# Graph attention on one core: scores of the first 32 tiles in groups of four instead of two

## The chip, the cores and the metric

The kernel runs on one core of one Trainium2 chip. The metric is the device time of one execution in microseconds (us). A core has a matrix engine (TensorE, PE in the profile; its weight loads are listed as PEld), a vector engine (DVE), an activation engine (ACT), GpSimd (POOL) and a queue that issues transfers (SP). Each takes its instructions in the order in which the program lists them, and they wait for one another by semaphores. Matrix products are accumulated in PSUM, which the program uses as eight banks of 128 partitions by 512 float32.

## The reference, cut to what matters

One graph attention layer with pre-normalisation, 384 nodes, 1024 features, 16 heads of 64:

```python
h = relu(layernorm(x))
q = h @ wq.T + bq;   k = h @ wk.T + bk;   v = h @ wv.T + bv
q2 = heads(q @ wiq.T + biq);  k2 = heads(k @ wik.T + bik);  v2 = heads(v @ wiv.T + biv)
scores = einsum('hnd,hmd->hnm', q2, k2) / 8 + mask        # mask from the edges, -inf elsewhere
out = einsum('hnm,hmd->hnd', softmax(scores), v2)
y = x + out.reshape(384, 1024) @ wo.T + bo
```

Everything is asked for in float32. The kernel makes each product out of three products of split operands: high part times high part, high times low, low times high.

## The kernel before, in words

The first part (up to about 158 us) makes the normalised input, the first projections, the mask and v2. The second part, which the change touches, is one loop over steps `i` from 0 to 59, written out by hand: the order in which the loop calls its functions is the order of the instructions on every engine. No scheduler moves them.

A **tile** is 128 rows of the scores of one head against all 384 columns. There are 48: head pair `p` (0 to 7), row block `t` (0 to 2), head `o` of the pair (0 or 1), so tile `i` has `p, r = divmod(i, 6)`, `t = r // 2`, `o = r % 2`. A tile passes through these functions:

- `do_S(i)`, in even steps, makes the scores of tiles `i` and `i+1` on PE: three product terms for two heads, six matmuls. A head has only 64 features, so its matmul uses 64 of the 128 rows of the array, and the two heads use the two halves (the profile writes 64\*128 for this form). The two results go to two banks of the tag "s", of which there are four, taken in turn.
- `do_ttr` (DVE, line 974) adds the mask out of the bank, writes the tile `e` and the row minimum. When it is done the bank is free. Step `i` calls it for tile `i-1`.
- `do_exp` (ACT) in step `i` for tile `i-2`; `do_recip` (DVE, then POOL); `do_high` (ACT, line 1009) for tile `i-5` and `do_low` (DVE, line 1013) for tile `i-6` make the two half-precision planes `pl`; `do_turn` transposes them by a transfer on the SP queue into `pt`.
- `av_mm(p)` (PE, line 1037) multiplies six turned tiles with v2: 18 matmuls that use 64 of the 128 columns of the array (128\*64). It is called in the steps of `a_at`: 14, 20, 26, ..., 50, 54. Where scores are made in that step it follows them directly, otherwise it comes later in the step.

PE's remaining time in the loop is filled by `fill`, which draws ordinary matmuls from two generators: the projections that make `iq` and `ik` of the next head pairs (lines 494 to 496, three matmuls to a piece; float16 operands for `iq`, 32-bit operands for `ik`), and later the output projection. Each step has a budget `r` in matmuls, `(STEP - costs of what the step does itself) / UNIT`; half is drawn ahead of `do_S`, half behind it. `STEP` is 1.94, `UNIT` 0.168, the cost of a score group `SMM` 0.7 and of `av_mm` `AMM` 1.69. The weights for these pieces are split on ACT, DVE (lines 118, 125, 127) and POOL (line 113) as the generators reach new chunks; the finished chunks are moved out of PSUM by ACT (lines 803, 807), DVE (804, 808) and POOL (809).

Of the kernel before, what the change touches and what calls it, by code (L numbers as in the profile page):

```python
# [19 lines left out]
N, D, NT, KT, NP = 384, 1024, 3, 8, 8  # L20
# [7 lines left out]
def gnn_kernel(ctx: ExitStack, tc: tile.TileContext, x, edges, erows, etw, wq, wk, wv, wiq, wik, wiv, wo,  # L28
# [6 lines left out]
    nc = tc.nc  # L35
# [14 lines left out]
    def bank(tag):  # L50
        return psum.tile([128, 512], F32, tag=tag, name=tag, bufs={"g": 3, "s": 4}.get(tag, 1))
# [742 lines left out]
    qk = {}  # L794
# [18 lines left out]
    def run_later():  # L813
        todo = later[:]
        later.clear()
        for f in todo:
            f()

    def run_tasks():
        while tasks:  # L820
            tasks.pop(0)()
# [54 lines left out]
    PRE, STEP, UNIT, SMM, AMM = 90, 1.94, 0.168, 0.7, 1.69  # L876
# [8 lines left out]
    def wo_prep(k):  # L885

        dst = None
        if k == 4:
            otile[0] = gtile("g3").rearrange("p a k n -> p (a k n)")
        if 4 <= k < 7:  # L890
            g, b = otile[0], (k - 4) * 2048
            dst = g[:, b:b + 2048]
        split_hi(WO + k, dst, k in ODVE)
        later.append(lambda: later.append(lambda: split_lo(WO + k)))
        load(WO + k + 3)
# [19 lines left out]
    def flush_y(n=6):  # L915
        for _ in range(min(n, len(ysums))):
            ysum(ysums.pop(0))
# [29 lines left out]
    def in_dma(i):  # L947
        return i < S - 2

    def tile_of(i):  # L950
        p, r = divmod(i, 6)
        return p, r // 2, r % 2

    st_ps, es, sts, tps, avs, aof = {}, {}, {}, {}, {}, {}
    S = 48
    TERMS = ((0, 0), (1, 0), (0, 1))

    def do_S(i):
        p, t, _ = tile_of(i)
        q, k = qk["iq", p], qk["ik", p]  # L960
        pair = [bank("s") for _ in range(2)]
        for j, (a, b) in enumerate(TERMS):
            for o in range(2):
                r = slice(o * 64, o * 64 + 64)
                nc.tensor.matmul(pair[o][:, :N], q[r, a, t * 128:(t + 1) * 128], k[r, b, :], start=(j == 0), stop=(j == 2))  # L965
        st_ps[i], st_ps[i + 1] = pair

    def do_ttr(i):
        t = tile_of(i)[1]
        e = es[i] = work.tile([128, N], F32, tag="e", name="e", bufs=EB)  # L970
        if i % 2 == 0:
            sts[i // 2] = work.tile([128, 6], F32, tag="s", name="s", bufs=5)
        s = sts[i // 2]
        nc.vector.tensor_tensor_reduce(e, st_ps.pop(i)[:, :N], ma[:, t, :], neg_c, 3.0e38, OP.add, OP.min,  # L974
                                       s[:, i % 2:i % 2 + 1])

    def do_exp(i):
        s, o = sts[i // 2], i % 2
        nc.scalar.activation(es[i], es[i], AF.Exp, bias=s[:, o:o + 1], scale=-1.0, accum_out=s[:, 2 + o:3 + o])  # L979
# [11 lines left out]
    def do_recip(i):  # L991
        s = sts[i // 2]
        nc.vector.reciprocal(s[:, 4:6], s[:, 2:4])  # L993
        if in_dma(i):
            nc.gpsimd.tensor_scalar(s[:, 4:6], s[:, 4:6], PSC, None, op0=OP.mult)  # L995

    def do_norm(i):
        if not in_dma(i):
            nc.gpsimd.tensor_tensor(es[i], es[i], factor(i).to_broadcast([128, N]), OP.mult)
# [7 lines left out]
    def do_high(i):  # L1007
        planes[i] = work.tile([128, 2, N], F16, tag="pl", name="pl", bufs=5)
        nc.scalar.activation(planes[i][:, 0, :], es[i], AF.Copy, scale=factor(i))  # L1009

    def do_low(i):
        pl = planes[i]
        nc.vector.scalar_tensor_tensor(pl[:, 1, :], es.pop(i), factor(i), pl[:, 0, :], op0=OP.mult, op1=OP.subtract)  # L1013

    def do_turn(i):
        pt, c = pt_of(i)
        nc.sync.dma_start_transpose(pt[:, :, c], planes.pop(i).rearrange("p a n -> p (a n)"))

    def turn_mm(i):
        ps = tps[i] = bank("s")  # L1020
        for k in range(3):
            nc.tensor.transpose(ps[:, k * 128:(k + 1) * 128], es[i][:, k * 128:(k + 1) * 128], ident)

    def do_pt(i):
        pt, c = pt_of(i)
        hi, lo = (pt[:, s * 3:s * 3 + 3, c] for s in range(2))
        pv = tps.pop(i)[:, :N].rearrange("p (k n) -> p k n", k=3)
        nc.scalar.activation(hi, pv, AF.Copy, scale=PSC)
        later.append(lambda: nc.vector.scalar_tensor_tensor(lo, pv, PSC, hi, op0=OP.mult, op1=OP.subtract))

    def av_mm(p):
        ps = avs[p] = bank("a")
        for k in range(3):
            for j, (sv, sp) in enumerate(TERMS):
                for o in range(2):
                    h = 2 * p + o
                    nc.tensor.matmul(ps[o * 64:o * 64 + 64, :N], vhl[:, k, h, sv, :], ptv[h % 4][:, 3 * sp + k, :],  # L1037
                                     start=(k == 0 and j == 0), stop=(k == 2 and j == 2))

    def do_ao(p):  # L1040
        f = aof[p] = work.tile([128, 512], F32, tag="aof", name="aof", bufs=3)[:, :N]
        nc.scalar.activation(f, avs.pop(p)[:, :N], AF.Identity, scale=0.5 / PSC, bias=bias_ao[:, p:p + 1])

    def do_aos(p):
        nc.vector.tensor_copy(ao[:, 0, p, :], aof[p])
        nc.gpsimd.tensor_tensor(ao[:, 1, p, :], aof[p], ao[:, 0, p, :], OP.subtract)
# [4 lines left out]
    def fill(n):  # L1051
        credit[0] += n
        while credit[0] > 0 and gens:
            try:
                c = next(gens[0])
            except StopIteration:
                gens.pop(0)
                continue
            if c == 0:
                credit[0] = 0.0  # L1060
                return
            credit[0] -= c
# [6 lines left out]
    t_at = {i + 5: i for i in range(S) if not in_dma(i)}  # L1069
    a_at = {6 * p + 14 if p < 7 else 54: p for p in range(8)}  # L1070
    for i in range(S + 12):
        now[0] = i
        scores = i < S and i % 2 == 0
        r = (STEP - SMM * scores - AMM * (i in a_at) - 0.33 * (i in t_at)) / UNIT
        fill(r / 2)
        if scores:
            do_S(i)
            if i in a_at:
                av_mm(a_at[i])
        fill(r / 2)  # L1080
        for o in range(2):
            x = i - LAGL[o]
            if x % 2 == o and 0 <= x < S and in_dma(x):
                do_low(x)
        if 0 <= i - 1 < S:
            do_ttr(i - 1)
        run_later()
        if 0 <= i - 2 < S:
            do_exp(i - 2)
        if 0 <= i - 3 < S and i % 2 == 0:  # L1090
            do_recip(i - 3)
            for x in (i - 4, i - 3):
                do_norm(x)
        for o in range(2):
            x = i - LAGH[o]
            if x % 2 == o and 0 <= x < S and in_dma(x):
                do_high(x)
        if i in t_at:
            turn_mm(t_at[i])
        if i in a_at and not scores:  # L1100
            av_mm(a_at[i])
        if i - 1 in t_at:
            do_pt(t_at[i - 1])
        if i - 1 in a_at:
            do_ao(a_at[i - 1])
        if i - 2 in a_at:
            do_aos(a_at[i - 2])
        run_tasks()
        for f in steps.pop(i, []):
            f()  # L1110
        for o in range(2):
            x = i - LAGT[o]
            if x % 2 == o and 0 <= x < S and in_dma(x):
                do_turn(x)
        if i in WSTEPS:
            wo_prep(wp)
            wready[wp] = i + 3
            wp += 1
        flush_y()
# [58 lines left out]
```

## Time and profile before

| | us |
|---|---|
| time, median of 3 runs | 277.41 (276.87 to 277.54) |
| the profiled execution's own time | 275.86 |
| its span, first to last instruction | 273.7 |
| PE busy | 267.6 |
| DVE busy | 230.5 |
| ACT busy | 215.2 |
| POOL busy | 136.7 |
| granted TensorE clock | 1.000 of full |

The profiled execution was 1.55 us shorter than the median of the runs; 2.16 us of its time lie outside the span. In the profile a row of the timeline gives start, duration, engine, line, operation, what is written from what, and how many instructions are merged into the row. Matmuls overlap, so the time that one takes on PE is read from its start to the next one's start, not from its duration. "64\*128 64x384 f16" means that 64 rows and 128 columns of the array are used, with an operand of 64 partitions by 384 elements in float16. Where an engine stood idle before an instruction, the row ends with that time and with what ended it.

### The profile page before, as it was taken

How to read it: one execution, taken by the hardware profiler on the slowest of the kernel's cores; microseconds unless marked ns; L12 is line 12 of the kernel's file. 1: busy time of each engine (PE TensorE's matmuls, PEld its weight loads, DVE VectorE, ACT ScalarE, POOL GpSimd, SP SyncE). 2: the span in 40 equal slices, each digit the busy share in tenths (PEclk: the TensorE clock that was granted, in tenths of full speed). 3: DMA queues.
4: the chain of work that ended last, by engine and by line, in shares of the span. 5: the costliest groups of instructions: out<-in, count | busy, mean ns of one | idle time of the engine just before them, and what ended most of it. 6: DMA issues, size and time to landing. Idle time of an engine off the chain costs nothing.

```text
span 273.7 us, 5038 instructions
## 1 busy us (share of the span) xinstructions
PE 267.6 (98%) x1626; PEld 186.9 (68%) x1626; DVE 230.5 (84%) x564; ACT 215.2 (79%) x417; POOL 136.7 (50%) x161
## 2 busy tenths in 40 slices
PE   7899999999999999999999999999999999999994
PEld 6899999999974444566668767766576664444543
DVE  4858986999999976798997899989988898999633
ACT  3797687599896977899968599979989899888400
POOL 4765754645778564868960005656574512212410
PEclk9999999999999999999999999999999999999999
DMA  7899999889989999396899953799899989999406
GB/s 257 267 299 406 387 397 392 323 282 403 369 261 355 383 312 341 104 379 250 288 375 393 411 209 119 172 206 211 168 240 164 216 197 167 201 174 136 86 14 219
DMA packets 58090, 72.05 MB, mean 263 GB/s; under 512 B 41040, under 2 KB 42576, under 8 KB 58064
## 3 DMA queue, kind: packets, MB, share of 16 engines
q1 hardware_dynamic: 56000, 69.93, 83.9%
q0 software_dynamic: 2064, 1.80, 2.1%
q8 instruction: 13, 0.21, 0.3%
q14 instruction: 13, 0.11, 0.1%
HBM read 59.27 MB, written 3.39 MB: 229 GB/s over the span
## 4 chain that ended last, share of the span: by engine, by line
PE 94%; DMA 2%; DVE 2%; ACT 0%; issue 0%; SPq 0%
PE g L494 24%; PE g L496 23%; PE g L495 23%; PE s L965 5%; PE a L1037 5%; PE s L494 3%; PE s L496 3%; PE s L495 3%; DMA g<-in_x_dram 2%; PE g L598 2%; PE a L495 1%; PE a L494 1%; PE a L496 1%; DVE whl L125 1%; DVE lnt L374 0%; ACT whl L102 0%
## 5 line engine op out<-in xcount | busy, mean ns | idle before, releaser
L494 PE MATMUL g<-g,whl 128*128 128x384 f32 (+1 forms) x248 | 85.3, 344 | 0.0
L496 PE MATMUL g<-g,whl 128*128 128x384 f32 (+1 forms) x248 | 82.6, 333 | 0.0
L495 PE MATMUL g<-g,whl 128*128 128x384 f32 (+1 forms) x248 | 82.5, 333 | 0.0
L351 POOL DMA_INDIRECT tab<-edge x51 | 61.9, 1213 | 37.5 <-DMA tab<-edge 23.5
L102 ACT ACTIVATE whl<-raw,small 128x1024 f16<-128x1024 f32 (+1 forms) x36 | 34.6, 970 | 3.9 <-DVE small L573 3.1
L494 PEld LDWEIGHTS g<-g,whl 128*128 128x128 f32 x184 | 34.5, 188 | 4.1 <-issue 3.1
L1013 DVE SCALAR_TENSOR_TENSOR pl<-e,s,pl 128x384 f16<-128x384 f32 x46 | 31.4, 683 | 7.0 <-ACT pl L1009 7.0
L125 DVE SCALAR_TENSOR_TENSOR whl<-raw,small,whl 128x1024 f16<-128x1024 f32 x24 | 32.8, 1368 | 4.6 <-ACT whl L102 3.6
L495 PEld LDWEIGHTS g<-g,whl 128*128 128x128 f32 x184 | 34.6, 188 | 0.0
L496 PEld LDWEIGHTS g<-g,whl 128*128 128x128 f32 x184 | 34.5, 188 | 0.0
L979 ACT ACTIVATE e<-e,s 128x384 f32<-128x384 f32 x48 | 29.1, 606 | 2.6 <-DVE s L974 2.5
L974 DVE CUSTOM_DVE_ANT_0 e<-s,ma,small 128x384 f32<-128x384 f32 x48 | 29.2, 608 | 0.0
L1009 ACT ACTIVATE pl<-e,s 128x384 f16<-128x384 f32 x46 | 27.8, 605 | 1.8 <-POOL s L995 1.7
L108 ACT ACTIVATE whl<-raw 128x1024 fp32r<-128x1024 f32 (+1 forms) x30 | 25.2, 847 | 2.4 <-DMA raw<-in_wik_dram 1.3
L995 POOL TENSOR_SCALAR s<-s 128x2 f32<-128x2 f32 x23 | 9.0, 393 | 34.4 <-DVE s L993 34.4
L127 DVE TENSOR_TENSOR whl<-raw,whl 128x1024 fp32r<-128x1024 f32 x17 | 21.0, 1237 | 2.4 <-ACT whl L108 2.1
L113 POOL TENSOR_TENSOR whl<-raw,whl 128x256 fp32r<-128x256 f32 x20 | 17.0, 858 | 9.3 <-issue 6.2
L155 ACT ACTIVATE scan<-scan 128x1024 f32<-128x1024 f32 x20 | 20.9, 1043 | 0.0
L494 PE MATMUL g<-hk,whl 128*128 128x384 f16 x64 | 20.9, 326 | 0.0
L495 PE MATMUL g<-hk,whl 128*128 128x384 f16 x64 | 20.9, 326 | 0.0
L496 PE MATMUL g<-hk,whl 128*128 128x384 f16 x64 | 20.9, 326 | 0.0
L809 POOL TENSOR_TENSOR ik<-f,ik 128x384 f16<-128x384 f32 x7 | 6.4, 913 | 28.2 <-DVE ik L808 23.6
(196 smaller groups left out, 552.0 us busy)
## 6 DMA issues: line engine op xcount, KB each, us to landing
raw<-in_wv_dram SPq DMA_DIRECT2D x8, 512.0 KB
raw<-in_wq_dram SPq DMA_DIRECT2D x8, 512.0 KB
scan<-in_wiv_dram SPq DMA_DIRECT2D x8, 512.0 KB
raw<-in_wiv_dram SPq DMA_DIRECT2D x8, 512.0 KB
scan<-in_wk_dram SPq DMA_DIRECT2D x8, 512.0 KB
raw<-in_wk_dram SPq DMA_DIRECT2D x8, 512.0 KB
g<-in_wo_dram SPq DMA_DIRECT2D x8, 512.0 KB
raw<-in_wiq_dram SPq DMA_DIRECT2D x8, 512.0 KB
```

What stands on the lines that cost most here:

```text
L102: soon(j if parts > 1 else -1, lambda c=c: nc.scalar.activation(hi[:, c], raw[w][:, c], AF.Copy, scale=sc))
L108: soon(j if parts > 1 else -1, lambda c=c: nc.scalar.activation(hi[:, c], raw[w][:, c], AF.Copy))
L125: nc.vector.scalar_tensor_tensor(lo, raw[w], sc, hi, op0=OP.mult, op1=OP.subtract)
L127: (eng or nc.vector).tensor_tensor(lo, raw[w], hi.bitcast(F32), OP.subtract)
L351: nc.gpsimd.indirect_dma_start(out=tabs[c // RNG], out_offset=bass.IndirectOffsetOnAxis(ap=idx[:, c:c + 1], axis=0), in_=val[:, c:c + 1], ...
L494: nc.tensor.matmul(ps, lhi, rhi, start=first, stop=False)
L495: nc.tensor.matmul(ps, lhi, rlo, start=False, stop=False)
L496: nc.tensor.matmul(ps, llo, rhi, start=False, stop=last)
L974: nc.vector.tensor_tensor_reduce(e, st_ps.pop(i)[:, :N], ma[:, t, :], neg_c, 3.0e38, OP.add, OP.min, s[:, i % 2:i % 2 + 1])
L979: nc.scalar.activation(es[i], es[i], AF.Exp, bias=s[:, o:o + 1], scale=-1.0, accum_out=s[:, 2 + o:3 + o])
L1009: nc.scalar.activation(planes[i][:, 0, :], es[i], AF.Copy, scale=factor(i))
L1013: nc.vector.scalar_tensor_tensor(pl[:, 1, :], es.pop(i), factor(i), pl[:, 0, :], op0=OP.mult, op1=OP.subtract)
```

## The change

For the first 32 tiles the scores are made in groups of four tiles, in every fourth step: twelve matmuls in a row into all four "s" banks. From tile 32 on nothing differs in the group size. For the first 32 tiles `do_ttr` is called one step earlier (tile `i` in step `i`); step 32 has none, and from step 33 on it is tile `i-1` again. The budget of `fill` is adapted in these steps: 0.05 less a step, and 0.49 more for a score group.

```diff
+    QUADS = 32
+
     def do_S(i):
-        p, t, _ = tile_of(i)
-        q, k = qk["iq", p], qk["ik", p]
-        pair = [bank("s") for _ in range(2)]
-        for j, (a, b) in enumerate(TERMS):
-            for o in range(2):
-                r = slice(o * 64, o * 64 + 64)
-                nc.tensor.matmul(pair[o][:, :N], q[r, a, t * 128:(t + 1) * 128], k[r, b, :], start=(j == 0), stop=(j == 2))
-        st_ps[i], st_ps[i + 1] = pair
+        for x in range(i, i + (4 if i < QUADS else 2), 2):
+            p, t, _ = tile_of(x)
+            q, k = qk["iq", p], qk["ik", p]
+            pair = [bank("s") for _ in range(2)]
+            for j, (a, b) in enumerate(TERMS):
+                for o in range(2):
+                    r = slice(o * 64, o * 64 + 64)
+                    nc.tensor.matmul(pair[o][:, :N], q[r, a, t * 128:(t + 1) * 128], k[r, b, :], start=(j == 0), stop=(j == 2))
+            st_ps[x], st_ps[x + 1] = pair
...
-        scores = i < S and i % 2 == 0
-        r = (STEP - SMM * scores - AMM * (i in a_at) - 0.33 * (i in t_at)) / UNIT
+        scores = i < S and i % (4 if i < QUADS else 2) == 0
+        r = (STEP - (i < QUADS) * 0.05 - (SMM + 0.49 * (i < QUADS)) * scores - AMM * (i in a_at) - 0.33 * (i in t_at)) / UNIT
         fill(r / 2)
         if scores:
             do_S(i)
...
-        if 0 <= i - 1 < S:
+        if i < QUADS:
+            do_ttr(i)
+        elif QUADS < i <= S:
             do_ttr(i - 1)
```

## The prediction

> **What bounds the kernel now.** I read the page first: the share of each engine and the chain that ended last.
>
> ```profile
> span 273.7 us, 5038 instructions
> ...
> PE 267.6 (98%) x1626; PEld 186.9 (68%) x1626; DVE 230.5 (84%) x564; ACT 215.2 (79%) x417; POOL 136.7 (50%) x161
> ...
> PE 94%; DMA 2%; DVE 2%; ACT 0%; issue 0%; SPq 0%
> ```
>
> PE is busy for 98% of the span and is 94% of the chain: whatever shortens PE's sequence shortens the run, as long as no other engine makes PE wait. The view of waits tells whether one does now.
>
> ```profile
> PE g L435 <- POOL ident masks.py:199: 1.4, 1, 1.4
> PE g L415 <- DVE g L407: 0.8, 1, 0.8
> PE s L415 <- ACT g L403: 0.2, 1, 0.2
> PEld L965 <- issue: 7.4, 24, 0.4
> ```
>
> PE's only named waits are three at the very start. None is for a score bank, for weights or for a turned tile. But its weight loads stood idle ahead of every one of the 24 score groups, 7.4 us in all, "until issue", so for nothing another engine did. Third, the share of the other engines in the stretch of the first 32 tiles:
>
> ```profile
> 160.00:216.00 56.00, 56.00 (x380) 37.30 (x379) 50.85 (x133) 50.80 (x120) 30.36 (x41) 1.00 0.89 188
> ```
>
> The columns are the stretch, its length, then busy time of PE, PEld, DVE, ACT, POOL, the clock, the DMA share and GB/s. PE has no gap. DVE and ACT have 5.15 and 5.20 us of slack in 56, and the clock is full.
>
> **The price of a score group.** Fourth, PE's timeline around score groups (line 965), one between float16 matmuls, one between 32-bit ones, and one that runs into `av_mm` (line 1037):
>
> ```profile
> 161.62 0.33 PE L495 MATMUL g<-g,whl 128*128 128x384 f16 x1
> 161.78 0.33 PE L496 MATMUL g<-g,whl 128*128 128x384 f16 x1
> 162.04 0.66 PE L965 MATMUL s<-ik,iq 64*128 64x384 f16 x6
> 162.63 0.34 PE L494 MATMUL g<-g,whl 128*128 128x384 f16 x1
> 162.80 0.33 PE L495 MATMUL g<-g,whl 128*128 128x384 f16 x1
> ...
> 165.36 0.33 PE L495 MATMUL g<-g,whl 128*128 128x384 f32 x1
> 165.53 0.34 PE L496 MATMUL g<-g,whl 128*128 128x384 f32 x1
> 165.80 0.66 PE L965 MATMUL s<-ik,iq 64*128 64x384 f16 x6
> 166.40 0.44 PE L494 MATMUL g<-g,whl 128*128 128x384 f32 x1
> 166.67 0.33 PE L495 MATMUL g<-g,whl 128*128 128x384 f32 x1
> ...
> 185.40 0.66 PE L965 MATMUL s<-ik,iq 64*128 64x384 f16 x6
> 185.99 1.65 PE L1037 MATMUL a<-pt,vhl 128*64 128x384 f16 x18
> 187.57 0.44 PE L494 MATMUL g<-g,whl 128*128 128x384 f32 x1
> ```
>
> From start to start an ordinary matmul takes 0.163 us in float16 (161.62 to 161.78, rounded) and 0.173 with 32-bit operands (165.36 to 165.53). Against that:
>
> - Entry: the last ordinary matmul ahead of a group takes 0.26 or 0.27 instead (161.78 to 162.04, 165.53 to 165.80), 0.10 too much each time.
> - Body: six score matmuls take 0.59 (162.04 to 162.63). The two heads run at once in the two halves of the array, so this is three pairs at 0.163, or 0.49, and 0.10 beside it.
> - Exit into a 32-bit matmul: that one takes 0.27 (166.40 to 166.67), 0.10 too much. Exit into a float16 one costs nothing (162.63 to 162.80 is 0.17).
>
> Is the body's 0.10 paid once a group or once per pair of banks? `av_mm` answers: 18 matmuls, nine pairs, take 1.58 (185.99 to 187.57), which is 9 x 0.163 = 1.47 and 0.11. The extra does not grow with the number of pairs; it is paid when the array changes its form. So I take a group of four at 0.59 + 3 x 0.163 = 1.08; the other end is 2 x 0.59 = 1.18.
>
> The page "TensorEngine Tiling (Array Packing)" of the Trainium skill, under Tiling Modes (Key Properties), says that a change of tiling mode drains the array, while a change of tile within a mode does not; the rows agree, at about 0.10 us for each change. The same page, under Performance Considerations (Instruction Overhead), speaks against: about 60 cycles for each matmul. If the body's 0.10 were that, a larger group would save none of it, and the sum below would be 0.7 instead of 1.5; the row of `av_mm` bears this out badly.
>
> **The change part by part.** *Order on PE.* The budget over four steps is 2 x (1.94 - 0.7) + 2 x 1.94 = 6.36 before and 4 x 1.89 - 1.19 = 6.37 after, so the ordinary matmuls stay the same in number and, to within one piece of three, in place. Worked out over the loop, the matmuls between one group of four and the next are 39, 36, 39, 27, 36, 30, 30 and 36, with `av_mm` in the stretches that start at tiles 12, 20 and 24.
>
> *Removed.* 16 groups become 8. Before: 16 x (0.10 + 0.10) = 3.2, and six of the 16 run into a 32-bit matmul (tiles 4, 8, 10, 16, 22, 28), 6 x 0.10 = 0.6: 3.8 in all. After: 8 x 0.20 = 1.6, and five exits into a 32-bit matmul (tiles 0, 4, 8, 16, 28), 0.5.
>
> *Added on PE.* In steps 14 and 26 `av_mm` no longer follows scores and stands alone between ordinary matmuls: two entries more. No lone `av_mm` is priced in these rows; the ends are 0 (as it is behind scores) and 0.10 (the entry of a score group). I take 0.10, as the form of the array changes there as well: 0.2.
>
> Sum: 3.8 - 1.6 - 0.5 - 0.2 = **1.5 us off PE's sequence**, nearly all between 158 and 220 us.
>
> *Moved on DVE: the row minima a step earlier.* No instruction is added; `do_ttr` of tile `i` now takes the place that tile `i-1` had, ahead of that step's weight splits and behind `do_low`. What is queued behind it on DVE is `do_recip` and the next `do_low`, and behind those POOL's scaling, ACT's `do_high` and the transposes on the SP queue; these keep their steps. On the SP queue, early loads of weights change place with one transpose; those loads are three chunks ahead of use, and the trace has no PE wait for weights.
>
> *Added waits.* There are two. First, the group starting at tile `4k` needs all four banks, so the minimum of tile `4k-1` must be done, half a group (0.5 us) after the group starts. Second, `do_ttr` of tile `4k` now stands in DVE's queue at the step in which its scores are made, and DVE may get there first.
>
> The first wait is a ring: scores, four minima with all that lies between, scores. Its length comes from DVE's rows, one start of a minimum to the end of the third after it, at the tiles that take those places:
>
> ```profile
> 196.12 0.61 DVE L974 CUSTOM_DVE_ANT_0 e<-s,ma,small 128x384 f32<-128x384 f32 x1
> ...
> 202.58 0.09 DVE L974 DVE_READ_ACCUMULATOR2_ANT s<- 128x1 f32 x1
> 203.18 0.60 DVE L974 CUSTOM_DVE_ANT_0 e<-s,ma,small 128x384 f32<-128x384 f32 x1
> ...
> 205.71 0.62 DVE L1013 SCALAR_TENSOR_TENSOR pl<-e,s,pl 128x384 f16<-128x384 f32 x1 [1.28 <-ACT pl L1009]
> ```
>
> From 196.12 to 202.58 are 6.46 us; with 0.65 for the first pair of scores ahead (0.59 and an estimate of 0.06 for the hand-over) and 0.5 off because the last two banks are needed later, the ring is 6.6 us. PE's shortest quad is 36 matmuls, 12 of them 32-bit: 1.08 + 12 x 0.173 + 24 x 0.163 + 0.20 = 7.3; the others are 7.5 to 8.0. The ring fits with 0.7 us to spare at the least. I cost it at nothing, under the cover of DVE's slack above.
>
> The second wait: where DVE is now against PE is seen from a score group and the place in DVE's queue that the first minimum will take.
>
> ```profile
> 173.84 0.66 PE L965 MATMUL s<-ik,iq 64*128 64x384 f16 x6
> 205.64 0.66 PE L965 MATMUL s<-ik,iq 64*128 64x384 f16 x6
> ```
>
> At tile 24 the place is reached at 203.18 and the scores are there at 205.64 + 0.6 = 206.2: DVE waits 3 us. But it waited 1.28 at that place already, for `do_high` (205.71), and it is early because it has slack. Every microsecond that PE gains takes one off this wait. It costs nothing as long as DVE's idle time, 5.15 less the 1.5 that PE gains, covers the work displaced.
>
> *The first quad* is the tightest place. Its minima start behind the mask, and `ik` of head pair 1 is needed in the group at tile 4 instead of tile 6:
>
> ```profile
> 163.16 0.62 DVE L974 CUSTOM_DVE_ANT_0 e<-s,ma,small 128x384 f32<-128x384 f32 x1
> 164.15 0.91 POOL L809 TENSOR_TENSOR ik<-f,ik 128x384 f16<-128x384 f32 x1 [22.69 <-DVE ik L808]
> ```
>
> Three minima at 0.54 from 163.16, the cast that feeds POOL (0.27), the fourth: done at 165.7. POOL then has the low part of `ik` at 165.1 + 0.9 = 166.0. PE's group at tile 4 starts near 165.7, wants the last two banks at 166.2 and that low part, the last term, at 166.5. Both hold, by 0.4 to 0.5 us. Cost nothing; at the other end some 0.5 us of PE wait, once.
>
> *Behind tile 32* PE arrives 1.5 us earlier at the output projection's weights. The tightest place there:
>
> ```profile
> 234.57 1.28 DVE L125 SCALAR_TENSOR_TENSOR whl<-raw,small,whl 128x1024 f16<-128x1024 f32 x1
> 235.88 0.38 PE L494 MATMUL g<-whl,g 128*128 128x512 f16 x1
> 236.10 0.38 PE L495 MATMUL g<-whl,g 128*128 128x512 f16 x1
> ```
>
> This split ends at 235.85 and the second matmul of its piece, which reads the low part, starts at 236.10. If DVE did not come forward with PE, up to 1.3 us would be lost here. DVE does come forward in my reckoning: its chain up to there hangs on evacuations that wait for PE, and it has one minimum (0.54) less behind step 32. Cost nothing; the bound for the range is 1.3.
>
> **The sum.** Against the profiled execution: 275.86 - 1.5 = 274.4. The median of the runs shown is 277.41, 1.55 above the profiled one; the same saving gives 275.9. About 0.3%, 0.83 us, is what a measurement of this kernel can tell from no change.
>
> **Rivals.**
>
> *The saving is half as large or half given back* (within 0.3%). Either a pair of banks costs 0.59 in a group of four too: 8 x 0.10 = 0.8 less, gain 0.7, 276.7. Or PE waits at the first quad (0.5) and at the output weights (up to 1.3, of which half, 0.65), gain 0.35, 277.1. For it: the small margins in the last two fences. Against: `av_mm`'s body, and the slack of 5 us.
>
> *Slower: the ring of four banks becomes the bound.* With all four banks in one group there is no spare bank; PE stands at the second half of a group until DVE has done the fourth minimum. The page "TensorEngine Tiling (Array Packing)" of the Trainium skill warns of this under Restrictions and Gotchas (PSUM Pressure) and under Performance Considerations (PSUM Bottleneck); no run here has yet shown it. It decides where the ring exceeds PE's quad, 7.6 on the mean: at 7.8 (0.19 x 8 = 1.5) the gain is gone. DVE's wait of up to 3 us for tile `4k`, if added to the wait for `do_high` instead of taking its place, would do that: 6.6 + 1.3 = 7.9, and 0.3 x 8 = 2.4, less 1.5, is 0.9: 278.3. Against: the wait for `do_high` hangs on ACT, which does not wait for the new order.
>
> **How the numbers follow.** The forecast (gain 0.9 to 2.2) gets 0.64, as its terms come from rows that agree among themselves; the half gain 0.20; the ring 0.16. So faster 0.64, same 0.20, slower 0.16. The low end 275.2 is the sum plus the remaining five exits and 0.2 for runs; the high end 278.2 takes in the half gain and most of the ring. The forecast's own range is 275.2 to 276.6.
>
> **What would show it.** In the profile after: eight rows of twelve score matmuls, each 1.08 from its start to the next matmul's start (1.18 would be the rival); entries still 0.10; the list of PE's waits without a row for scores against the minima (with one, the ring); DVE rows that wait for scores, some us in all, and fewer of the waits for `do_high`; `av_mm` in step 14 with an entry of 0.10. Wrong would be a PE wait for `ik` from POOL near 166 us, or for a split of the output weights near 234.

## The result, and the profile after

The changed kernel takes 275.80 us (median of 23 runs) against 277.25 us before (23 runs); the ratio is 0.9953, with a 95% interval of 0.9937 to 0.9969. It is 1.3 us faster (0.9 to 1.7), where 1.5 was forecast, and the time forecast was 275.9.

The first profile of the changed kernel has a wait of 3.1 us of PE ahead of the changed stage (line 187, for a maximum over weights that arrived late: ACT waits 3.65 us for their transfer, 1.61 before). The lines below are from a second profile of the same kernel; the changed stage is alike in both to 0.01 us. In five of the twelve profiles used here, the first one among them, the granted clock is 0.78 to 0.88 between 150 us and the first score matmul, but from there to the last matmul it is 1.00 in all. Page, shares and chain of the second profile:

```profile
span 274.0 us, 5038 instructions
...
PE 266.2 (97%) x1626; PEld 188.0 (69%) x1626; DVE 233.1 (85%) x564; ACT 214.4 (78%) x417; POOL 138.1 (50%) x161
...
PE 11%; ACT 4%; DVE 4%; issue 3%; POOL 1%; DVEq 0%; ACTq 0%; POOLq 0%
```

The chain, 94% PE before, is now followed through PE for only 11% of the span: from the end back it leaves PE at a wait behind tile 32, goes into DVE and ACT, and cannot be followed beyond about 209 us, so its shares don't add up to the whole. So more than PE's sequence sets the end now. The waits (engine and line, what was waited for, total, times, longest), all of PE's and two others:

```profile
PE g L187 <- DVE small L182: 1.7, 1, 1.7
PE g L435 <- POOL ident masks.py:199: 1.4, 1, 1.4
PE s L415 <- ACT g L403: 0.4, 1, 0.4
PE g L495 <- DVE whl L125: 0.3, 1, 0.3
PE g L494 <- DVE iq L804: 0.3, 1, 0.3
...
PEld L968 <- issue: 5.3, 16, 0.4
...
DVE e L977 <- PE s L968: 2.5, 2, 1.9
```

Of PE's waits only the one at line 495 lies in the changed stage or behind it. The wait at line 187 is 0 in the profile before and 1.1 to 4.6 us in seven of the ten profiles below, with the same order of instructions up to there. Times of whole runs scatter by it, so the experiments below are read mainly from one stretch: from the start of the first score matmul to the start of the last matmul of the kernel. The rows at its ends, before:

```profile
269.92 0.27 PE L496 MATMUL g<-whl,g 128*128 128x256 f16 x1
```

which with 158.41 for the first group gives 111.51, and after:

```profile
159.05 0.34 PE L496 MATMUL g<-g,whl 128*128 128x384 f32 x1
159.32 1.15 PE L968 MATMUL s<-ik,iq 64*128 64x384 f16 x12
160.40 0.44 PE L494 MATMUL g<-g,whl 128*128 128x384 f32 x1
...
185.89 0.34 PE L496 MATMUL g<-g,whl 128*128 128x384 f32 x1
186.16 1.65 PE L1040 MATMUL a<-pt,vhl 128*64 128x384 f16 x18
187.74 0.44 PE L494 MATMUL g<-g,whl 128*128 128x384 f32 x1
...
270.22 0.27 PE L496 MATMUL g<-whl,g 128*128 128x256 f16 x1
```

That is 110.90 (159.32 to 270.22). The first group of the changed kernel stands three 32-bit matmuls (0.52 us) earlier in PE's order, so 110.38 compares with 111.51: 1.13 us saved in the stretch. The same rows show the prices: a group of four from its start to the next matmul's takes 1.08 (159.32 to 160.40), its entry 0.27 instead of 0.17 (159.05 to 159.32), and the lone `av_mm` of step 14 also has an entry of 0.27 (185.89 to 186.16).

Where the stretch divides, at the group of tile 32 (220.32 before, 220.63 after): the first part takes 61.91 before and 61.31 after, and in the changed kernel it holds six 32-bit matmuls more (the three that now come behind the first group, and three moved ahead of tile 32; 1.04 us). So the first 32 tiles gained 1.64. The second part takes 49.60 before and 49.59 after, with the three matmuls fewer, 0.52: behind tile 32, 0.51 were given back. Nearly all of this is lost at one place. From DVE's and PE's timelines:

```profile
235.07 1.28 DVE L125 SCALAR_TENSOR_TENSOR whl<-raw,small,whl 128x1024 f16<-128x1024 f32 x1
...
235.69 0.38 PE L494 MATMUL g<-whl,g 128*128 128x512 f16 x1
236.41 0.38 PE L495 MATMUL g<-whl,g 128*128 128x512 f16 x1 [0.34 <-DVE whl L125]
```

It is the place named in the prediction (a split of the output weights). From start to start the two matmuls are 0.72 apart, before 0.22 (235.88 to 236.10): 0.50 lost. The view shows 0.34 of it, as it counts from the end of the matmul ahead, which is 0.38 long. Counted from the first group the split ended at 77.44 before (235.85 less 158.41) and ends at 76.51 now (236.35 less 159.32 and 0.52), 0.93 us earlier. PE gained 1.64, and before the matmul came 0.25 behind the split; what is left, 0.46, is about what PE loses. What is open is why DVE came forward by less than PE.

### The profile page after: what moved, and what is told of

Same layout as the page of the kernel before. It is cut to its first block, busy times and chain, and to the rows that moved or that the text cites. A ratio compares the mean times of both kernels' runs of the same rounds, so it can differ in the third digit from the quotient of the medians.

```text
span 277.1 us, 5038 instructions
## 1 busy us (share of the span) xinstructions
PE 267.1 (96%) x1626; PEld 188.6 (68%) x1626; DVE 229.2 (83%) x564; ACT 214.6 (77%) x417; POOL 137.5 (50%) x161
## 5 line engine op out<-in xcount | busy, mean ns | idle before, releaser
L351 POOL DMA_INDIRECT tab<-edge x51 | 60.4, 1185 | 38.4 <-DMA tab<-edge 22.1
L1016 DVE SCALAR_TENSOR_TENSOR pl<-e,s,pl 128x384 f16<-128x384 f32 x46 | 32.7, 711 | 4.4 <-ACT pl L1012 4.2
L125 DVE SCALAR_TENSOR_TENSOR whl<-raw,small,whl 128x1024 f16<-128x1024 f32 x24 | 32.2, 1342 | 4.2 <-ACT whl L102 3.9
L998 POOL TENSOR_SCALAR s<-s 128x2 f32<-128x2 f32 x23 | 10.4, 452 | 32.7 <-DVE s L996 31.4
L809 POOL TENSOR_TENSOR ik<-f,ik 128x384 f16<-128x384 f32 x7 | 7.8, 1114 | 33.6 <-DVE ik L808 28.7
L155 ACT ACTIVATE g<-g 128x1024 f32<-128x1024 f32 x16 | 16.7, 1046 | 6.4 <-DMA g<-in_wik_dram 6.4
```

The lines of the kernel that those rows point to most:

```text
L125: nc.vector.scalar_tensor_tensor(lo, raw[w], sc, hi, op0=OP.mult, op1=OP.subtract)
L155: nc.scalar.activation(x, x, AF.Square if n in ("k", "iq", "ik") else AF.Abs, accum_out=l1[:, SROW[n], k:k + 1])
L351: nc.gpsimd.indirect_dma_start(out=tabs[c // RNG], out_offset=bass.IndirectOffsetOnAxis(ap=idx[:, c:c + 1], axis=0), in_=val[:, c:c + 1], ...
```

## The experiments

The theories: **A**, the gain is the changes of the array's form that PE saves, at 0.10 us each. **B**, it comes from the earlier row minima. **C**, the ring of four banks holds PE. **D**, formed after the first four runs: DVE's waits for fresh scores delay what stands behind them and so ACT, and this gives part of the gain back behind tile 32. Every run of a group was compared with the kernel before on the same chip. All stretches but those of the groups of two are measured from the earlier first group; against the kernel before, 0.52 is taken off.

### The changed kernel again

No edit.

> The changed kernel again, for a profile at full clock and as the reference of the other runs. Theory A (the gain is the changes of the array's form saved on PE: 0.10 us at the entry of a group, 0.10 in its body, 0.10 at an exit into a 32-bit matmul): 1.3 to 1.5 us faster than the kernel before, eight rows of twelve score matmuls at 1.08, no wait of PE for a minimum. Theory C (the ring of four banks holds PE at times): PE waits for line 977 somewhere between 160 and 220 us.

Measured: ratio 0.9965 (0.9929 to 1.0002), which takes in A's 1.3 to 1.5 us and also no gain; its profile is shown above. Theory A holds in its prices: eight rows of twelve score matmuls, each 1.08. There is no wait of PE for a minimum, against C.

### Groups of two, with the earlier minima alone

```diff
-        if 0 <= i - 1 < S:
-            do_ttr(i - 1)
+        if i < 32:
+            do_ttr(i)
+        elif 32 < i <= S:
+            do_ttr(i - 1)
```

> The kernel before, groups of two throughout, with the row minima alone moved a step earlier for the first 32 tiles. PE's order is that of the kernel before. Theory A: no change, within 0.3 us of the kernel before, as PE did not wait for a bank. Rival B (part of the gain comes from the minima being earlier, which frees banks and feeds ACT sooner): at least 0.5 us faster than the kernel before.

Measured: 0.5% slower, 1.0049 (1.0015 to 1.0082). Neither A's no change nor B's gain. The stretch is 112.90, 1.39 longer; the first 32 tiles take 61.91 as before, to 0.01, so all of it is lost behind them. From the timelines of DVE and PE:

```profile
221.54 0.62 DVE L974 CUSTOM_DVE_ANT_0 e<-s,ma,small 128x384 f32<-128x384 f32 x1 [0.70 <-PE s L965]
222.08 0.08 DVE L974 DVE_READ_ACCUMULATOR2_ANT s<- 128x1 f32 x1
222.08 0.35 DVE L808 CAST ik<-f 128x384 f16<-128x384 f32 x1
222.35 1.28 DVE L125 SCALAR_TENSOR_TENSOR whl<-raw,small,whl 128x1024 f16<-128x1024 f32 x1
223.55 0.16 DVE L993 RECIPROCAL s<-s 128x2 f32<-128x2 f32 x1
...
241.21 0.38 PE L495 MATMUL g<-whl,g 128*128 128x512 f16 x1 [1.25 <-DVE whl L125]
```

DVE stands at the minimum of tile 30 for scores that PE has not made; the cast, the split and the reciprocal, which need nothing from these scores, stand behind it. Six such waits sum to 4.8 us in this profile. In the first 85 us of the stretch ACT waits 9.1 us for POOL's scaled reciprocals, in the kernel before 1.0. PE then stands 1.25 us at the split of line 125; from start to start (239.58 to 241.21) it loses 1.41 there, the whole difference. B falls, and with it the view that the move is free: theory D.

### A group of four with ordinary matmuls in its middle

```diff
         for x in range(i, i + (4 if i < QUADS else 2), 2):
+            if x == i + 2:
+                fill(3)
...
-        fill(r / 2)
+        fill(r / 2 - 3 * (scores and i < QUADS))
```

> The changed kernel with one piece of three ordinary matmuls taken from behind a group of four and put between its two pairs (this happens in seven of the eight groups); bank use, minima and budget stay. Counted over PE's order: 7 entries and 7 bodies more than the changed kernel and three exits more into a 32-bit matmul, 17 x 0.10 = 1.7. Theory A: 1.7 us slower than the changed kernel, so about 0.2 slower than the kernel before. Rival B (the gain has to do with the banks and the earlier minima, not with the form): still 1 us or more faster than the kernel before.

Measured: 1.0034 (0.9991 to 1.0077); stretch 112.51, 1.61 longer than in the changed kernel, where A said 1.7 and B nothing. The first 32 tiles alone are 1.76 longer; behind them PE, which now comes later, waits less for line 125. One of the split groups:

```profile
163.82 0.34 PE L496 MATMUL g<-g,whl 128*128 128x384 f32 x1
164.10 0.66 PE L970 MATMUL s<-ik,iq 64*128 64x384 f16 x6
164.69 0.44 PE L494 MATMUL g<-g,whl 128*128 128x384 f32 x1
164.97 0.33 PE L495 MATMUL g<-g,whl 128*128 128x384 f32 x1
165.14 0.34 PE L496 MATMUL g<-g,whl 128*128 128x384 f32 x1
165.41 0.66 PE L970 MATMUL s<-ik,iq 64*128 64x384 f16 x6
166.00 0.34 PE L494 MATMUL g<-g,whl 128*128 128x384 f16 x1
```

Entry, body and exit are paid twice: 0.28 into the first half and 0.27 into the second, 0.59 for each half, 0.28 for the 32-bit matmul between. With the same banks and minima the gain is gone. It is a price of the changes of form. What the array does in that time the runs don't show: the weight loads stand idle about 0.3 us ahead of each score group (7.4 us at 24 groups, 5.3 at 16), and whether a load that comes late or the array itself takes the 0.10 is open, as is why an exit into a float16 matmul is free.

### Groups of four for all 48 tiles

```diff
-    QUADS = 32
+    QUADS = 48
```

> The changed kernel with groups of four for all 48 tiles. Counted over PE's order: 3 entries, 4 bodies and one exit less, 0.8 us. Theory A: 0.8 us faster than the changed kernel. Theory C: from 220 us on DVE is 90 to 97% busy and PE has fewer ordinary matmuls between the groups, so the ring is longer than PE's quad there; PE waits for minima (line 977) at the groups of tiles 36, 40 and 44, and the run is no faster, or slower, than the changed kernel.

Measured: 0.9962 (0.9925 to 0.9999), not told apart from the changed kernel; stretch 111.71, 0.81 *longer* than there, while the count on PE is 0.8 shorter. Theory C's outcome, but not its place: no PE wait for a minimum, and instead

```profile
237.41 0.38 PE L495 MATMUL g<-whl,g 128*128 128x512 f16 x1 [1.26 <-DVE whl L125]
...
260.42 2.85 PE L1040 MATMUL a<-pt,vhl 128*64 128x384 f16 x18
```

The wait for the split is 0.92 longer than in the changed kernel. The last `av_mm` is drawn out too; there it is

```profile
259.85 2.09 PE L1040 MATMUL a<-pt,vhl 128*64 128x384 f16 x18
```

so 0.76 is lost in it. With the 0.8 saved, 0.92 and 0.76 give 0.88 longer, where 0.81 was measured.

### The two lone `av_mm` put behind groups of four

```diff
-    a_at = {6 * p + 14 if p < 7 else 54: p for p in range(8)}
+    a_at = {6 * p + 14 + 2 * (p in (0, 2)) if p < 7 else 54: p for p in range(8)}
```

> The changed kernel with the two lone av_mm (steps 14 and 26) put behind the next group of four (steps 16 and 28). Counted over PE's order: two entries and four exits into 32-bit matmuls less, 6 x 0.10 = 0.6 on PE. Theory A: the stretch from the first score matmul to the last matmul is 0.6 us shorter than in the changed kernel (110.9 us there). Theory D (behind about tile 24 PE no longer sets the pace: DVE and ACT do, through the wait of DVE for fresh scores, so what PE gains is given back at the split of the output weights): the first 32 tiles are 0.6 shorter, and PE waits that much longer at line 125's split.

Measured: 0.9986 (0.9959 to 1.0012); stretch 111.20, 0.30 longer. The first 32 tiles take 61.38, no gain there either, for here the ring does hold PE, in the middle of the group of tile 20:

```profile
195.82 0.82 PE L968 MATMUL s<-ik,iq 64*128 64x384 f16 x7
197.00 0.64 PE L968 MATMUL s<-ik,iq 64*128 64x384 f16 x5 [0.36 <-DVE s L977]
```

```profile
192.29 0.85 DVE L118 SCALAR_TENSOR_TENSOR whl<-raw,small,whl 128x512 f16<-128x512 f32 x1
...
194.47 0.74 DVE L118 SCALAR_TENSOR_TENSOR whl<-raw,small,whl 128x512 f16<-128x512 f32 x1
...
196.33 0.60 DVE L977 CUSTOM_DVE_ANT_0 e<-s,ma,small 128x384 f32<-128x384 f32 x1
196.87 0.08 DVE L977 DVE_READ_ACCUMULATOR2_ANT s<- 128x1 f32 x1
```

The fourth minimum ends at 196.9 and the next score matmul starts right behind it. From this group to the next, with the same matmuls between, 8.64 us pass (195.82 to 204.46) against 7.96 in the changed kernel: 0.68 for a wait of 0.36. (The wait is counted from the end of the seventh matmul, 0.32 us long; the eighth would have started together with it.) The 0.6 saved on PE went there. Behind tile 32 PE waits 0.56 for line 125 instead of 0.34, which is theory D's place. So C is real here. It is hardly that PE came too early: its way from the group of tile 16 (at 188.59, in the changed kernel at 190.03) is 7.23 instead of 7.30. DVE's is longer: from that group to the end of the fourth minimum 8.34 pass instead of 6.15. With `av_mm` out of step 14 nine more ordinary matmuls are drawn ahead of tile 16 (36 instead of 27), and two splits of line 118 now stand ahead of this minimum. In the changed kernel both follow it, and the minimum is done 1.65 us before the bank is wanted (196.18 against 197.33 + 0.50):

```profile
195.58 0.60 DVE L977 CUSTOM_DVE_ANT_0 e<-s,ma,small 128x384 f32<-128x384 f32 x1
...
196.12 0.74 DVE L118 SCALAR_TENSOR_TENSOR whl<-raw,small,whl 128x512 f16<-128x512 f32 x1
```

### The first minimum of a group held back

The minima of a group of four come as none, one, one, two over its steps; the first never stands in DVE's queue before its scores.

```diff
         if i < QUADS:
-            do_ttr(i)
+            for x in ((), (i - 1,), (i - 1,), (i - 1, i))[i % 4]:
+                do_ttr(x)
```

> The changed kernel with the minima of a group of four given out as none, one, one, two over its four steps instead of one in each: the first minimum never stands in DVE's queue before its scores are there, the last one stays where it was. PE's order is that of the changed kernel. Theory D (DVE's waits for fresh scores, 2.5 us in that profile, hold back the scaling and with it ACT, and cost the 0.3 to 0.5 us that PE loses behind tile 32): DVE's waits for line 968 vanish, ACT's waits for POOL's scaling (3.5 us) shrink, PE's waits for the split of line 125 and for line 804 go, 0.3 to 0.6 us faster than the changed kernel. Theory A alone (these waits only take the place of other idle time): no change.

Measured: stretch 110.55, 0.35 shorter than in the changed kernel, with the first 32 tiles at 61.32 and no PE wait shown in the stretch. A second run of it, below, gave 110.57. The two matmuls at the split of line 125 are 0.37 apart instead of 0.72, so 0.35 of the 0.50 lost there are back and 0.15 are not. The chain that theory D claims stands in the rows of the changed kernel (DVE, POOL, ACT):

```profile
205.98 0.62 DVE L977 CUSTOM_DVE_ANT_0 e<-s,ma,small 128x384 f32<-128x384 f32 x1 [1.89 <-PE s L968]
...
206.80 0.16 DVE L996 RECIPROCAL s<-s 128x2 f32<-128x2 f32 x1
...
206.96 1.28 POOL L809 TENSOR_TENSOR ik<-f,ik 128x384 f16<-128x384 f32 x1 [2.28 <-DVE s L996]
208.22 0.65 POOL L998 TENSOR_SCALAR s<-s 128x2 f32<-128x2 f32 x1
...
208.90 0.61 ACT L1012 ACTIVATE pl<-e,s 128x384 f16<-128x384 f32 x1 [1.88 <-POOL s L998]
```

ACT's waits in the first 85 us of the stretch, first the changed kernel, then this one:

```profile
ACT pl L1012 <- POOL s L998: 4.2, 7, 1.9
ACT e L982 <- DVE s L977: 2.8, 4, 1.2
ACT f L807 <- PE g L496: 0.7, 1, 0.7
```

```profile
ACT f L807 <- PE g L496: 5.8, 6, 1.7
ACT e L982 <- DVE s L977: 1.6, 3, 0.5
ACT pl L1012 <- POOL s L998: 1.3, 3, 0.6
ACT iq L803 <- PE g L496: 1.0, 1, 1.0
```

In the changed kernel ACT waits for the scaled reciprocals, which stand in DVE's queue behind the waiting minimum, and hardly ever for PE: it has lost its lead. Here DVE's waits for scores are gone and ACT waits for PE again. The 5.8 us are not firm: this profile has a wait of 4.6 us ahead of the stage, and the second one, with 1.1 there, has 2.7; ACT's wait for the scaling is 1.3 in both. Theory D holds, at the low end of its 0.3 to 0.6. The wait for line 804 that the expectation names lies ahead of the stage (at 151.67 in the changed kernel) and is there again in the second run, so it is no part of this. The times do not settle it: the ratio was 0.9990 (0.9952 to 1.0028) in this group and 0.9871 (0.9830 to 0.9912) in the later one, on another chip.

### The same for all 48 tiles

```diff
-    QUADS = 32
+    QUADS = 48
...
-            do_ttr(i)
+            for x in ((), (i - 1,), (i - 1,), (i - 1, i))[i % 4]:
+                do_ttr(x)
```

> The same order of minima with groups of four for all 48 tiles; PE's order is that of the earlier run with 48, counted at 0.8 us less than the changed kernel, which was given back by a wait of 1.3 us for a split of line 125. Theory D: with the waits for scores gone PE's wait for line 125 shrinks from 1.3 to 0.5 us or less, and the run is 0.5 to 1.0 us faster than the changed kernel. Rival (DVE and ACT are simply full between 224 and 240 us): PE waits 1 us or more at the same place.

Measured: 0.9986 (0.9958 to 1.0013), stretch 111.22: 0.49 shorter than the other run with 48, still 0.32 longer than the changed kernel. PE's wait is 0.89 instead of 1.26:

```profile
235.86 0.38 PE L495 MATMUL g<-whl,g 128*128 128x512 f16 x1 [0.89 <-DVE whl L125]
```

Between D (0.5 or less) and its rival (1 or more): there the waits for scores are one part, and the load of DVE and ACT ahead of the output weights another, which I did not take apart. The last `av_mm` loses 0.65 here as well, with a wait of 0.43 for the turned tile (line 1032). The 0.8 saved, 0.55 more at line 125 and these 0.65 make 0.40 longer, against 0.32 measured: the gain that 48 tiles would bring is lost at these two places, and D explains only a part of the first.

### Both, and one `av_mm` alone

Held-back minima with both `av_mm` moved, and with only that of step 26 moved; the second differs from the first by

```diff
-    a_at = {6 * p + 14 + 2 * (p in (0, 2)) if p < 7 else 54: p for p in range(8)}
+    a_at = {6 * p + 14 + 2 * (p == 2) if p < 7 else 54: p for p in range(8)}
```

> The late order of minima and the two av_mm behind groups of four, groups of four for the first 32 tiles. Sum of the two: 0.6 on PE and the 0.3 to 0.6 given back. Theory A with D: 0.9 to 1.2 us faster than the changed kernel. If DVE and ACT are full: 0.5 or less.

> Groups of four for the first 32 tiles, minima in the order none, one, one, two, and of the two lone av_mm only the one of step 26 put behind the next group of four (step 28); the one of step 14 stays, since moved to 16 it shortened the way to the group of tile 20 and PE stood there for the fourth minimum. Counted over PE's order: one entry and two exits less, 0.3 us. Theory A with the ring: no PE wait for line 977, the stretch from the first score matmul to the last matmul 110.2 to 110.3 us (110.55 with the late minima alone, 110.90 in the changed kernel). If the ring also holds at tile 28 or 32: a PE wait there and 110.6 or more.

Measured: with both, 0.9951 (0.9910 to 0.9992), stretch 111.05, 0.15 longer than the changed kernel where 0.9 to 1.2 less was forecast. PE waits 0.2 for the fourth minimum in the group of tile 20 again, which takes 0.80 (8.76 to the next group instead of 7.96), though DVE has no wait for scores left; and 0.3 for line 125. With one, 0.9873 (0.9821 to 0.9926), median 274.87; no PE wait for a minimum, and the first 32 tiles take 61.01, the counted 0.3 less. But the stretch is 110.55, as without the move: behind tile 32 the 0.3 are given back at line 125 (PE waits 0.3 there). The forecast of 110.2 to 110.3 was wrong by what DVE and ACT take back. Its reason for leaving step 14 alone, a shorter way of PE to tile 20, is not what the rows above show: it was DVE's longer way.

The held-back minima alone, run again beside it, without an edit:

> The late minima once more, for a second profile and a narrower ratio. The profile's stretch from the first score matmul to the last matmul again 110.5 to 110.6 us, 0.35 less than in the changed kernel, with no wait of PE in it; the time 1.3 to 1.7 us below the kernel before, if the stretch is what sets it.

Measured: 0.9871 (0.9830 to 0.9912), median 274.90, 274.19 to 275.32; stretch 110.57, as forecast, with no PE wait shown in it. The time is 3.1 us below the kernel before by the medians, not 1.3 to 1.7: the stretch is not all that sets it.

## Why the prediction was right

- *PE bounds the kernel.* Right in the first 32 tiles. Behind them it was on the edge, which the empty list of PE's waits did not show; the prediction's own rows did (a split that ends at 235.85, a matmul that starts at 236.10).
- *The price of a group and of four.* Right: 1.08 for a group of four, 0.10 at each entry, at each exit into a 32-bit matmul, and in a body whatever its length. The split groups gave 1.61 back where the count of these prices said 1.7. The rival of 1.18 a group falls, and with it the reading that the body's 0.10 is an overhead of each matmul. The rule that a change of tiling mode drains the array, in "TensorEngine Tiling (Array Packing)" of the Trainium skill, Tiling Modes, agrees with these rows; that the 0.10 is such a drain no run here shows.
- *The lone `av_mm`.* Right: its entry costs 0.10.
- *The sum on PE*, 1.5: measured 1.64 in the first 32 tiles.
- *The ring.* Right that it fits, and about right in its margin of 0.7: from the end of the fourth minimum to the eighth matmul of the next group the changed kernel has 0.55 at tile 4 and 0.81 to 2.36 at tiles 8 to 28. Its first term, 0.65 from a group's start to the minimum that stands ready for it, is 0.69 here (205.29 to 205.98). But the length holds for this order alone: moving an `av_mm` by two steps put 2.2 us into DVE's part and made PE stand at tile 20.
- *The first quad.* Right, no wait; the 0.55 at tile 4 is its margin, forecast at 0.4 to 0.5.
- *The second wait, DVE for fresh scores, costed at nothing.* This term was mis-sized. It was named with what stands behind it (the scaling, ACT's `do_high`), but I took it to replace DVE's wait for `do_high`. For DVE it did: in the first 85 us its waits for `do_high` fell from 6.1 to 3.2, with 2.5 of waits for scores beside them, 1.9 in one piece. But these stand ahead of the reciprocal and so hold ACT back, and with the minima held back 0.35 of the 0.51 us lost behind tile 32 return. In groups of two the same move costs 1.39, with nothing to set against it.
- *Behind tile 32, costed at nothing, bound 1.3.* It cost 0.51. The bound held, but the reckoning that DVE comes forward with PE did not: it came forward by 0.93 of 1.64. The PE wait for a split of the output weights that the prediction named as a sign of being wrong is there.

The two errors cancel only in part: 1.5, 0.14 more on PE and 0.51 less behind it make 1.13 in the stretch. That the time forecast, 275.9, lies 0.1 from the median is partly luck: the whole runs gained 1.3 (0.9 to 1.7), from a reference 0.16 lower than the one the forecast started from.

## What to carry to other kernels

Where the matrix engine changes between full and half-array matmuls, count the changes, not the matmuls: here each cost about 0.10 us however many matmuls stood between, so fewer and longer groups saved a fixed sum each. When a consumer is moved earlier in an in-order queue, look at what stands behind it that needs nothing of its input; a wait there that the waiting engine can afford may still take the lead from the next engine. An engine without waits in a profile may be a few tenths of a microsecond from one: before a gain is counted in full, look for the nearest handover downstream. And a block of matmuls that is moved takes other work along: what is drawn in its place pulled two weight splits ahead of a minimum that PE needed.

## What the runs showed that I had not expected

That the earlier minima alone make the kernel slower by 1.4 us without touching the 61.91 us of the stage in which they lie; all of it shows at one matmul, some 15 us behind the last of the early minima. That a wait of 0.36 in the middle of a score group costs 0.68. And that the same kernel (held-back minima) gave ratios of 0.9990 and 0.9871 in two groups of runs while its stretch was 110.55 and 110.57. The groups ran on two chips; the medians of the kernel before were 277.05 and 278.04 there, those of this kernel 275.69 and 274.90. The difference lies outside the changed stage, and I did not find where.
